# Key tiles of a graph-attention kernel: cast once and kept in DRAM, instead of cast anew in each of seven query chunks

## The chip, the cores and the metric

The kernel runs on one core of a Trainium2 chip. A core has TensorE (PE), VectorE (DVE), ScalarE (ACT), GpSimd (POOL) and SyncE (SP), each with its own in-order instruction queue; here nearly all DMAs are issued from SP's queue. Time is the device time of one execution in microseconds (us). The kernel before took 10917.11 us, the median of three runs (10916.01 to 10922.77).

## The reference

Four graph layers stand one after another over N = 3327 nodes with 128 features and a dense 0/1 adjacency matrix. The first and third multiply by the adjacency, the last adds a nearest-neighbour step. Nearly all the time is spent in the second, an attention whose logits get the adjacency added twice:

```python
h = Wq.shape[0] // d
q = (x @ Wq.T).reshape(d, n, h)
k = (x @ Wk.T).reshape(d, n, h)
v = (x @ Wv.T).reshape(d, n, h)
a = jnp.einsum('dnh,dmh->dnm', q, k) * scale
a = a + spatial_encoding + edge_encoding      # both are adj
a = jax.nn.softmax(a, axis=2)
out = jnp.einsum('dnm,dmh->dnh', a, v)
out = out.reshape(n, h * d)
return out @ Wo.T
```

With d = 128 and h = 8 there are 128 attention maps of 3327 x 3327 logits, each with a contraction over only 8 numbers: 1.4 billion exponentials.

## The kernel before, in words

**Tiling of the attention.** The queries are cut in 7 chunks of QW = 476 columns (the last has 471, worked as 472). The 128 maps are taken four at a time, which makes 32 groups. The 3327 keys are cut in T = 26 tiles of 128. One step is (chunk c, group g, tile t); the loop runs over 7 x 32 x 26 = 5824 steps with t innermost, and two steps make a pair. The order of every engine's instructions in this loop is the program's own (a manual schedule): nothing is reordered, and each queue runs ahead as far as its waits let it.

**Keys.** A product of fp32 precision is made from parts: each key row is split in a high and a low part, and four maps' parts lie on 4 x 32 partitions. In chunk 0 the class `Parting` does that on POOL for the group after next (L582, L583: `hi` and `lo`), tile by tile of t from 2 to 9, and stores the parts to DRAM (`kt` for keys, `qt` for queries). `load_keys(g)` then brings a group's keys into `k_in`, 128 partitions x 3328, with eight DMAs of 16 partitions (L606), after a memset on POOL of the last column (L601). The pool `kq` holds two such tiles. A node's place in `k_in` is node = 26 p + t, so the 128 keys of a tile t are strided, and TensorE needs the type F32R. `key_pair` (L638) therefore casts two tiles at a time from `k_in` to a small tile `k` of 128 x 2 x 128, contiguous, of which there are nine buffers; casts run seven pairs ahead of their use. This is done in all seven chunks, for the same 32 groups of keys each time. The cast is on DVE, but on POOL at t = 5, and at t = 17 where POOL has an addition to a degree sum to do (`beside`).

**A pair of steps** (`scores`). PE makes eight products of 32 x 128 by 32 x 476 (L852), four for the even tile into four `early` banks, three for the odd tile into `late` and one more `early`. DVE adds the doubled adjacency `a2` to five of them (L855, from PSUM into the tile `p8` in SBUF). For the others PE adds it in PSUM with a product by 2I (L871, one of three, two of three in chunk 0 for t below 10) or POOL multiplies by exp(a2) after the exponential (L875). ScalarE takes the exponential twice: of the three late results (L873) and of the five that DVE wrote (L876). Six steps later `weigh` multiplies with the values on PE (L883). After a group's last step DVE copies the sums `acc` to `o4` (L892, seen at t = 5 of the next group), and four DMAs store them.

**The rest of the loop.** At t = 8 the next group's queries and values are loaded (`load_rest`, L628 and L613), at t = 14 the keys of the group after the next (`load_keys`). Adjacency tiles of the next chunk are loaded at t = 6 and doubled by POOL at t = 22 (L282); each is added to a degree sum at t = 17 of the next group (L293). In group 0 of each later chunk, at t = 19, `store_sum` makes the degrees on PE (L297) after the last addition, and DVE scales them (L298). In the last group of a chunk ScalarE makes the 13 exponentials of the next chunk's odd adjacency tiles (`exp_of`).

**DMA.** SP's issues are spread in turn over eight semaphores, and each issue waits until the one eight before it has landed.

Of the kernel before, what the change touches and what calls it, by code (L numbers as in the profile page):

```python
# [8 lines left out]
F32 = mybir.dt.float32  # L9
F32R = mybir.dt.float32r  # L10
# [11 lines left out]
P = 128  # L22
N = 3327
D = 128
T = 26
NP = P * T
# [28 lines left out]
def kernel(  # L55
# [211 lines left out]
    vd = dpool.tile([GP, EA], F32, name="vd")  # L267
    ot = dpool.tile([EA, GP], F32, name="ot")
    adj16 = dpool.tile([T, P, N], BF16, name="adj16")

    q_chunks = chunks(N, QW)
    adj_pools = [ctx_at.enter_context(tc.tile_pool(name="at_adj0", bufs=T))]
# [324 lines left out]
                    self.store(side)  # L597

    def load_keys(g):
        k_in = kq.tile([P, NP], F32, name="k_in")  # L600
        nc.gpsimd.memset(k_in[:, N:], 0.0)  # L601
        for i in range(4):
            n0 = (4 * g + i) * N
            for j in range(2):
                r = 32 * i + HL * j
                nc.sync.dma_start(k_in[r : r + HL, :N], kt[:, n0 : n0 + N])  # L606
        return k_in

    def load_values(g):
        v4 = kq.tile([P, 4, T, EA], F32, name="v4")  # L610
# [119 lines left out]
    for g in range(2):  # L730
        raw = {}

        def keys(g=g, raw=raw):
            raw["k"] = kq.tile([P, NP], F32, name="k_in")
            nc.gpsimd.memset(raw["k"][:, N:], 0.0)
            load_raw(raw["k"], kf, g, N)

        def others(g=g, raw=raw):
            w = q_chunks[0][1]
            raw["q"] = side.tile([P, QW], F32, name="q_raw")  # L740
            load_raw(raw["q"], qf, g, w)
            raw["v"] = load_values(g)

        def parted(g=g, raw=raw):
            split_rows(raw["k"], raw["k"], NP, low_k)
            q4 = kq.tile([P, QW], F32R, name="q4")
            split_rows(q4, raw["q"], q_chunks[0][1], low_q)
            first.append((q4, raw["v"]))
            k_ins.append(raw["k"])

        early += [keys, others, parted]
# [77 lines left out]
    with tc.tile_pool(name="at_in", bufs=1) as a_pool, tc.tile_pool(name="at_p", bufs=4) as p_pool, tc.tile_pool(  # L829
# [16 lines left out]
        def scores(step, k, q4, a2, e_a, p8, n_g):  # L846
            c, _, t = step
            we = even(c)

            def product(i, sp, stop=True):  # L850
                r = slice(32 * i, 32 * i + 32)
                nc.tensor.matmul(sp[:, :we], k[r, t % 2, :], q4[r, :we], start=True, stop=stop)  # L852

            def add(i, sp):
                nc.vector.tensor_tensor(p8[:, PLACES[t % 2][i], :we], sp[:, :we], a2[:, :we], op=ALU.add)  # L855

            if t % 2 == 0:
                early = [ps.tile([P, 512], F32, name="early", bufs=4) for _ in range(4)]
                for i in range(4):
                    product(i, early[i])  # L860
                for i in range(4):
                    add(i, early[i])
                return
            n_i = 3 - n_g
            late = ps.tile([P, 3, 512], F32, name="late")
            early = ps.tile([P, 512], F32, name="early", bufs=4)
            for i in range(3):
                product(i, late[:, i], stop=i >= n_i)
            product(3, early)
            for i in range(n_i):  # L870
                nc.tensor.matmul(late[:, i, :we], two_i, a2[:, :we], start=False, stop=True)  # L871
            add(3, early)
            nc.scalar.activation(p8[:, 5:8, :we], late[:, :, :we], AF.Exp)  # L873
            g8 = p8[:, 8 - n_g : 8, :we]
            nc.gpsimd.tensor_tensor(g8, g8, e_a[:, :we].unsqueeze(1).to_broadcast([P, n_g, we]), op=ALU.mult)  # L875
            nc.scalar.activation(p8[:, :5, :we], p8[:, :5, :we], AF.Exp)  # L876
# [20 lines left out]
        with tc.manual_schedule(engines=engines):  # L897
# [4 lines left out]
            e_t, e_next = e_first, []  # L902
            to_store = [(0, t, a2) for t, a2 in enumerate(a_t)]
            begun, to_sum = {}, []
            for j, step in enumerate(steps):
                c, g, t = step
                n = c * n_groups + g + 1
                more = n < len(groups)
                if t == 0:
                    if j:  # L910
                        q4, v4 = coming
                        if g == 0:
                            a_t, a_next = a_next, []
                            e_t, e_next = e_next, []
                if t % 2 == 0:
                    p8 = p_pool.tile([P, 8, QW], F32, name="p8")
                parting = c == 0
                scores(step, pairs[j // 2], q4, a_t[t], e_t[t // 2], p8, 1 if parting and t < 10 else 2)
                begun[j] = (step, v4, p8)
                if j >= ahead:  # L920
                    weigh(*begun.pop(j - ahead))
                if t == 8 and more:
                    coming = first[n] if n < len(first) else load_rest(*groups[n])
                if parting:
                    if t == 0:
                        part = ahead_part
                    for due in range(t, t + 1 if t < T - 1 else max(T, 16)):
                        part.at(due)
                        if due == 15 and g + 1 < n_groups:
                            ahead_part = Parting((g + 3) % n_groups)  # L930
                            ahead_part.load(0)
                            ahead_part.load(1)

                beside = t == 17 and bool(to_sum)
                if beside:
                    while to_sum:
                        add_to_sum(*to_sum.pop(0))
                if t == 19 and g == 0 and c:
                    store_sum(c, ps.tile([P, 512], F32, name="early", bufs=4), a_pool.tile([P, QW], F32, name="o4"))
                if t % 2 and len(pairs) < len(steps) // 2:  # L940
                    key_pair(nc.gpsimd if t == ahead - 1 or beside else nc.vector, k_ins, pairs)
                if t == 14 and n + 1 < len(groups):
                    k_ins.append(load_keys(groups[n + 1][1]))
                if t == min(6, T // 2) and c + 1 < len(q_chunks):
                    for _ in range(min(len(to_store), 1 + T // n_groups)):
                        store_adj(*to_store.pop(0))
                    a_in = [load_adj(c + 1, i) for i in range(len(a_next), T * (g + 1) // n_groups)]
                if t == max(T - 4, 3) and c + 1 < len(q_chunks):
                    for a, i, w in a_in:
                        a_next.append(doubled(adj_pools[(c + 1) % 2], a[: rows_of(i), :w], i, w))  # L950
                        to_sum.append((a_next[-1], c + 1, i == 0))
                        to_store.append((c + 1, i, a_next[-1]))
                if t % 2 and g == n_groups - 1 and c + 1 < len(q_chunks):
                    e_next.append(exp_of(a_next[t], c + 1))
# [522 lines left out]
```

## Time and profile before

| what | value |
|---|---|
| median of the runs shown | 10917.11 us |
| the profiled execution's own time | 10917.88 us |
| its span in the trace | 10916.1 us, 202151 instructions |
| attention loop, first to last exponential | 432.6 to 10189 us of the span |
| PE busy | 10569.0 us (97%) |
| DVE busy | 10192.0 us (93%) |
| ACT busy | 10078.4 us (92%) |
| POOL busy | 7529.7 us (69%) |
| key loads (k_in from kt) | 1776 DMAs of 207.9 KB |
| DMA moved | 926.49 MB, 85 GB/s over the span |

A row of a group names line, engine, operation, the tiles written and read, shapes and count; behind the bar stand the busy time of the group in us, the mean of one instruction in ns, and the engine's idle time just before, with what ended it. In an extract in order of time the columns are start and duration in us, then the same names, and in brackets the idle time before with its releaser. Recorded durations of neighbours on one engine can overlap; then the distance of starts is what one costs. A matmul's busy time is not PE at its peak.

### The profile page before, as it was taken

Reading aid. Unit: us, or ns where it says so; the run is one execution under the profiler, and the core shown is the slowest. Engines: PE = TensorE matmul, PEld = TensorE weight load, DVE = VectorE, ACT = ScalarE, POOL = GpSimd, SP = SyncE. Lnnn points to the kernel's source line nnn. Section 1 sums busy time; section 2 is a strip of 40 time slices with the busy share of each in tenths; the row PEclk is TensorE's granted clock in tenths of the full one; section 3 lists DMA queues with packets and bytes.
Section 4 is the critical chain, followed back from the end, with each engine's and each line's share of the span. In section 5 each row is a group of like instructions: output and inputs, shape, how many; then the busy total and the mean of one; then the engine's idle time right before and its main releaser. Section 6 shows DMA issues by size and latency. Waiting matters only on the chain. (4 is left out here: it accounts for less than half of the span.)

```text
span 10916.1 us, 202151 instructions
## 1 busy us (share of the span) xinstructions
PE 10569.0 (97%) x76707; PEld 3105.4 (28%) x76740; DVE 10192.0 (93%) x17975; ACT 10078.4 (92%) x6276; POOL 7529.7 (69%) x4622
## 2 busy tenths in 40 slices
PE   7899999999999999999999999999999999999896
PEld 3322222222222222222222222222222222222453
DVE  5799999999999999999999999999999999999656
ACT  2799999999999999999999999999999999999432
POOL 3388887777777777777777777777777776666203
PEclk9999999999999999999999999999999999999998
DMA  8655554433433343334334333433343333333422
GB/s 299 203 126 123 122 121 110 69 63 65 71 63 63 65 72 63 63 65 71 63 65 70 64 62 65 70 65 63 64 70 64 64 60 63 56 61 60 148 101 100
DMA packets 420912, 926.49 MB, mean 85 GB/s; under 512 B 67976, under 2 KB 349567, under 8 KB 385882
## 3 DMA queue, kind: packets, MB, share of 16 engines
q1 hardware_dynamic: 416744, 906.95, 40.8%
q8 instruction: 606, 9.93, 0.4%
q0 software_dynamic: 3184, 6.51, 0.2%
q14 instruction: 378, 3.10, 0.1%
HBM read 773.47 MB, written 139.72 MB: 84 GB/s over the span
## 5 line engine op out<-in xcount | busy, mean ns | idle before, releaser
L855 DVE TENSOR_TENSOR p<-early,a 128x476 f32<-128x476 f32 (+1 forms) x14560 | 8412.0, 645 | 214.0 <-PE early L852 184.9
L875 POOL TENSOR_TENSOR p<-p,e 128x952 f32<-128x952 f32 (+2 forms) x2912 | 6325.4, 2172 | 2440.9 <-ACT p L873 2273.2
L876 ACT ACTIVATE p<-p 128x2380 f32<-128x2380 f32 (+1 forms) x2912 | 7099.5, 2438 | 0.0
L883 PE MATMUL acc<-p,v 128*9 128x476 f32 (+1 forms) x46592 | 5738.2, 564 | 28.0 <-DVE o L892 13.0
L873 ACT ACTIVATE p<-late 128x1428 f32<-128x1428 f32 (+1 forms) x2912 | 4675.3, 1606 | 33.1 <-PE late L871 30.0
L852 PE MATMUL early<-q,k 32*128 32x476 f32 (+1 forms) x14560 | 3699.5, 479 | 28.3 <-DVE p L855 5.0
L852 PEld LDWEIGHTS early<-q,k 32*128 32x128 f32 x14560 | 1567.6, 181 | 2764.0 <-DVE p L855 2708.9
L852 PE MATMUL late<-q,k 32*128 32x476 f32 (+1 forms) x8736 | 1415.9, 479 | 47.8 <-ACT p L873 47.7
L638 DVE CAST k<-k_in 128x256 fp32r<-128x256 f32 x2525 | 1335.9, 529 | 0.0
L852 PEld LDWEIGHTS late<-q,k 32*128 32x128 f32 x8736 | 547.6, 181 | 2373.2 <-ACT p L873 2156.5
L871 PE MATMUL late<-a,two_i 128*128 128x476 bf16 (+1 forms) x3072 | 1123.8, 374 | 0.0
L883 PEld LDWEIGHTS acc<-p,v 128*9 128x9 f32 x46592 | 692.5, 88 | 1351.9 <-issue 1256.4
L871 PEld LDWEIGHTS <-two_i 128*128 128x128 bf16 x3072 | 281.0, 96 | 664.8 <-issue 664.8
L638 POOL CAST k<-k_in 128x256 fp32r<-128x256 f32 x387 | 290.4, 751 | 0.0
L233 PE MATMUL agg_ps<-a,part 128*128 128x512 bf16 (+1 forms) x1067 | 226.7, 370 | 6.1 <-ACT agg L1261 3.2
L282 POOL TENSOR_SCALAR a<-a_in 128x476 bf16<-128x476 f32 (+2 forms) x156 | 225.3, 1444 | 0.5
L345 PE MATMUL agg_ps<-a,part 128*128 128x512 bf16 (+4 forms) x720 | 170.9, 395 | 51.6 <-DMA a<-in_adjT_dram 50.3
L293 POOL TENSOR_TENSOR deg_half<-deg_half,a 128x476 f32<-128x476 f32 (+1 forms) x175 | 212.4, 1213 | 2.1
L192 ACT COPY agg<-agg_ps 128x512 f32<-128x512 f32 x9 | 4.7, 594 | 196.1 <-PE agg_ps L233 196.1
L1256 PE MATMUL sp<-yT,hT 128*128 128x512 f32 (+1 forms) x364 | 171.1, 611 | 12.1 <-ACT agg L1261 6.2
L1172 POOL TENSOR_TENSOR xs_late<-xs_late,b_s 128x3328 f32<-128x3328 f32 x1 | 7.2, 7247 | 224.8 <-DVE ln_xc L162 224.8
L892 DVE COPY o<-acc 105x476 f32<-105x476 f32 (+1 forms) x224 | 144.6, 645 | 10.5 <-PE acc L883 9.1
(286 smaller groups left out, 2550.0 us busy)
## 6 DMA issues: line engine op xcount, KB each, us to landing
k_in<-kt SPq DMA_DIRECT2D x1776, 207.9 KB
v<-vd SPq DMA_DIRECT2D x896, 117.0 KB
a<-in_adjT_dram SPq DMA_DIRECT2D x39, 1663.5 KB
a<-adj SPq DMA_DIRECT2D x78, 831.8 KB
q<-qt SPq DMA_DIRECT2D x1520, 29.8 KB
a_in<-in_adjT_dram SPq DMA_DIRECT2D x125, 238.0 KB
adj<-a SPq DMA_DIRECT2D x156, 119.0 KB
vd<-v_st SPq DMA_DIRECT2D x25, 576.0 KB
```

Of the source, the lines that this page charges most:

```text
L233: nc.tensor.matmul(acc[c][:, :w], part[:, t, :], a[:, c0 : c0 + w], start=(t == 0 and i == 0), stop=(t == T - 1 and i == len(parts) - 1),)
L282: nc.gpsimd.tensor_scalar(a2[:kp, :w], a, 2.0, None, op0=ALU.mult)
L293: nc.gpsimd.tensor_tensor(deg_half[:, :w], deg_half[:, :w], a2[:, :w], op=ALU.add)
L638: engine.tensor_copy(k, slots(k_in)[:, t : t + 2, :])
L852: nc.tensor.matmul(sp[:, :we], k[r, t % 2, :], q4[r, :we], start=True, stop=stop)
L855: nc.vector.tensor_tensor(p8[:, PLACES[t % 2][i], :we], sp[:, :we], a2[:, :we], op=ALU.add)
L871: nc.tensor.matmul(late[:, i, :we], two_i, a2[:, :we], start=False, stop=True)
L873: nc.scalar.activation(p8[:, 5:8, :we], late[:, :, :we], AF.Exp)
L875: nc.gpsimd.tensor_tensor(g8, g8, e_a[:, :we].unsqueeze(1).to_broadcast([P, n_g, we]), op=ALU.mult)
L876: nc.scalar.activation(p8[:, :5, :we], p8[:, :5, :we], AF.Exp)
L883: nc.tensor.matmul(acc[32 * i : 32 * i + EA, :w], v4[:kp, i, t, :], p8[:kp, PLACES[t % 2][i], :w], start=(t == 0), stop=(t == T - 1),)
L1256: nc.tensor.matmul(sp[:, c0 : c0 + w], slots(zT)[:, t, :], z2T[:, cols], start=True, stop=False)
```

## The change

A DRAM scratch `keyd` holds, for each of the 32 groups, all 26 cast key tiles side by side (128 x 3328). In chunk 0 keys are loaded and cast as before, and each cast pair is also stored to `keyd` in one DMA of 128 rows of 1 KB, issued one pair after its cast; the seven pairs cast ahead of the loop are stored before it begins. From chunk 1 on a group's tiles come back from `keyd` in one DMA into a tile of `k_in`'s name and size, now of type F32R, issued at t = 4 of the group before; PE reads the tile t out of it directly, and `key_pair` and `load_keys` are not called. In chunk 0 the cast of t = 17 is now always on DVE.

```diff
+    keyd = dpool.tile([NH // 4, P, NP], F32, name="keyd")
 ...
-        k_in = kq.tile([P, NP], F32, name="k_in")
+        k_in = kq.tile([P, NP], F32R, name="k_in").bitcast(F32)
 ...
+    def load_tile_keys(g):
+        k = kq.tile([P, NP], F32R, name="k_in")
+        nc.sync.dma_start(k.bitcast(F32), keyd[g])
+        return k.rearrange("r (t p) -> r t p", p=P)
+
+    def store_tile_keys(n):
+        g, t = divmod(2 * n, T)
+        nc.sync.dma_start(keyd[g, :, t * P : (t + 2) * P], pairs[n].rearrange("r t p -> r (t p)").bitcast(F32))
 ...
-                nc.tensor.matmul(sp[:, :we], k[r, t % 2, :], q4[r, :we], start=True, stop=stop)
+                nc.tensor.matmul(sp[:, :we], k[r], q4[r, :we], start=True, stop=stop)
 ...
+            n_pairs = n_groups * T // 2
+            k_now, k_next = None, None
+            n_stored = len(pairs)
+            for n in range(n_stored):
+                store_tile_keys(n)
 ...
                         q4, v4 = coming
+                        k_now = k_next
 ...
-                scores(step, pairs[j // 2], q4, a_t[t], e_t[t // 2], p8, 1 if parting and t < 10 else 2)
+                k = pairs[j // 2][:, t % 2] if c == 0 else k_now[:, t]
+                scores(step, k, q4, a_t[t], e_t[t // 2], p8, 1 if parting and t < 10 else 2)
 ...
-                beside = t == 17 and bool(to_sum)
-                if beside:
+                if t == 17:
                     while to_sum:
                         add_to_sum(*to_sum.pop(0))
 ...
-                if t % 2 and len(pairs) < len(steps) // 2:
-                    key_pair(nc.gpsimd if t == ahead - 1 or beside else nc.vector, k_ins, pairs)
-                if t == 14 and n + 1 < len(groups):
+                if t % 2 and n_stored < len(pairs):
+                    store_tile_keys(n_stored)
+                    n_stored += 1
+                if t % 2 and len(pairs) < n_pairs:
+                    key_pair(nc.gpsimd if t == ahead - 1 else nc.vector, k_ins, pairs)
+                if t == 14 and n + 1 < n_groups:
                     k_ins.append(load_keys(groups[n + 1][1]))
+                if t == 4 and n_groups <= n < len(groups):
+                    k_next = load_tile_keys(groups[n][1])
```

More of the change, by code (lines that the diff above doesn't have):

```diff
@@ L733, in keys @@
         def keys(g=g, raw=raw):
-            raw["k"] = kq.tile([P, NP], F32, name="k_in")
+            raw["k"] = kq.tile([P, NP], F32R, name="k_in").bitcast(F32)
             nc.gpsimd.memset(raw["k"][:, N:], 0.0)
```

## The prediction

> **What bounds the kernel now.** I read the page first, then the sums of each engine by stretch, cut at the start of each chunk's first late exponential, then ScalarE's instructions in order of time, then DVE's and POOL's beside them. By stretch (columns: PE, weight loads, DVE, ScalarE, POOL busy us; granted clock; DMA share; GB/s), chunks 0, 1 and 6:
>
> ```profile
> 432.60:1844.30 1411.70, 1390.10 (x10531) 363.75 (x10531) 1364.77 (x2472) 1404.10 (x845) 1172.81 (x1069) 1.00 0.54 122
> 1844.30:3237.40 1393.10, 1377.63 (x10402) 372.58 (x10402) 1357.91 (x2472) 1390.52 (x846) 1034.38 (x559) 1.00 0.38 66
> 8813.70:10188.90 1375.20, 1369.30 (x10409) 371.59 (x10406) 1365.26 (x2485) 1372.60 (x833) 949.66 (x512) 1.00 0.35 56
> ```
>
> Three engines look full. Which one is, the order of time decides. The groups concerned:
>
> ```profile
> L876 ACT ACTIVATE p<-p 128x2380 f32<-128x2380 f32 (+1 forms) x2912 | 7099.5, 2438 | 0.0
> L873 ACT ACTIVATE p<-late 128x1428 f32<-128x1428 f32 (+1 forms) x2912 | 4675.3, 1606 | 33.1 <-PE late L871 30.0
> L638 DVE CAST k<-k_in 128x256 fp32r<-128x256 f32 x2525 | 1335.9, 529 | 0.0
> L638 POOL CAST k<-k_in 128x256 fp32r<-128x256 f32 x387 | 290.4, 751 | 0.0
> ```
>
> The last seven pairs of tiles have no cast, since casts run seven pairs ahead. ScalarE in chunk 6, first with casts on DVE, then without:
>
> ```profile
> 10100.03 1.95 ACT L873 ACTIVATE p<-late 128x1416 f32<-128x1416 f32 x1
> 10101.26 2.78 ACT L876 ACTIVATE p<-p 128x2360 f32<-128x2360 f32 x1
> 10103.32 1.95 ACT L873 ACTIVATE p<-late 128x1416 f32<-128x1416 f32 x1
> ...
> 10179.03 2.15 ACT L873 ACTIVATE p<-late 128x1416 f32<-128x1416 f32 x1
> 10180.26 2.98 ACT L876 ACTIVATE p<-p 128x2360 f32<-128x2360 f32 x1
> 10182.33 2.15 ACT L873 ACTIVATE p<-late 128x1416 f32<-128x1416 f32 x1
> ```
>
> Start to start a pair takes 3.29 us with the casts and 3.30 without. The starts count: recorded durations overlap. So ScalarE is the bound, at 3.319 us a pair (median spacing of L873's starts) in chunks 0 to 5 and 3.292 in the narrower chunk 6, and taking casts from DVE buys only what ScalarE loses against that floor.
>
> **What it loses.** Floor of chunks 1 to 5: 416 pairs x 3.319 = 1380.6, plus 13 more exponentials of the next chunk's tiles at 0.49 (the spacing in the last group is 3.81) = 6.4: 1387.0. Starts of the chunks give 1393.1, 1394.2, 1393.4, 1395.2, 1393.5; excess 6.1, 7.2, 6.4, 8.2, 6.5. Chunk 6: 1375.2 less 416 x 3.292 = 1369.3: 5.9. Together 40.3 us. Two parts:
>
> (a) One stall in each chunk's group 0, where PE's degree product (L297) waits for POOL's last addition and everything behind it on PE is late:
>
> ```profile
> 3267.28 1.75 ACT L873 ACTIVATE p<-late 128x1428 f32<-128x1428 f32 x1
> 3268.52 2.58 ACT L876 ACTIVATE p<-p 128x2380 f32<-128x2380 f32 x1
> 3274.19 1.36 ACT L873 ACTIVATE p<-late 128x1428 f32<-128x1428 f32 x1 [3.09 <-PE late L871]
> ```
>
> 6.91 less 3.32 = 3.59 here; over the six chunks 2.78, 3.59, 2.91, 4.75, 2.89, 3.04 = 20.0, and 0.28 each in the pairs after it, 1.6.
>
> (b) The other 18.7 us are delays of 0.1 to 0.3, mostly near t = 21. There DVE's cast meets POOL's multiplication:
>
> ```profile
> 2396.86 2.90 DVE L855 TENSOR_TENSOR p<-early,a 128x476 f32<-128x476 f32 x5
> 2399.66 1.35 DVE L638 CAST k<-k_in 128x256 fp32r<-128x256 f32 x1
> ...
> 2396.63 1.29 POOL L293 TENSOR_TENSOR deg_half<-deg_half,a 128x476 f32<-128x476 f32 x1
> 2397.86 0.68 POOL L638 CAST k<-k_in 128x256 fp32r<-128x256 f32 x1
> 2398.52 2.22 POOL L875 TENSOR_TENSOR p<-p,e 128x952 f32<-128x952 f32 x1
> ```
>
> The 964 casts of DVE with no POOL work beside them take 0.40; this one ends 0.27 after L875 does. Five additions 2.81 (start to start) and a free cast 0.33 make 3.14, 0.18 under ScalarE's 3.32; a cast of 1.35 makes 4.1.
>
> **The change part by part.** *Chunks 1 to 6, casts gone* (2525 + 387 now; 377 + 39 in the changed program). DVE falls to 2.81 a pair, slack 0.5, and part (b) should go: 18.7 at most, nothing at least; I take 17, since the late pairs are those of blocked casts. The 0.40 itself buys nothing: it lies beside ScalarE. In (a) the chain ScalarE, POOL L875, L293, PE L297 stays. Only its end shortens: in four chunks (1.44 each) DVE's cast of t = 19 sits between L298 and the additions that give PE a bank back, and PE's product waits some 0.6 for it (at 1878.81 the late products are out, the early one only at 1879.41): 4 x 0.6 = 2.4, and the 1.6 after it. Bounds 0 and 6 x 1.4 = 8.4; I take 4, from the PE row. Next late after DVE is that same stall, 16 to 20 us.
>
> *Chunks 1 to 6, the load.* Eight issues a group become one, bytes as before (1.70 MB). A 13,308-byte packet takes 1.5 us in the DMA records; 8 on each of 16 engines are 12 us. The issue waits for PE's last product on that buffer (two groups back) and stands behind the value loads, so about the group's start; PE needs it 43 us on. Behind it SP has stores and loads for the next group, up to 35 us early. Cost 0; cover 43 - 12 = 31 us. POOL loses 192 memsets of 0.1, hidden.
>
> *Chunk 0, the stores.* 416 of 131 KB (seven of them before the loop, where SP issues nothing from 427 to 442.6), each waiting on SP for a cast done a pair before. Issue: 0.35 (the row of the like adj<-a) to 0.75 (k_in<-kt), 13 a group, 4.6 to 9.8 us in SP's free stretch of about 17 (from 995 to 1012). Four stand ahead of the raw loads of the next parting: lo_k goes out at 992.8 and POOL first uses it at 1006.5, so 1.4 to 3 us later is covered. Data: 1,664 packets a group at some 0.06 (0.054 for 936 bytes) over 16 engines, 6.2 us, share 0.54 to about 0.68. A cast now waits for the store of nine pairs before, 30 us old; behind it on DVE stand the additions that ScalarE needs. The slowest backlog: the cast of t = 13 (981.1) is stored after lo_q, landing near 998, wanted at 1011. Cost 0, bounds 0 and the rival below.
>
> *Chunk 0, the cast of t = 17 moves* from POOL to DVE in 25 groups. Does it fit?
>
> ```profile
> 984.97 2.88 DVE L855 TENSOR_TENSOR p<-early,a 128x476 f32<-128x476 f32 x5
> 988.36 2.89 DVE L855 TENSOR_TENSOR p<-early,a 128x476 f32<-128x476 f32 x5 [0.52 <-PE early L852]
> ...
> 985.17 2.23 POOL L875 TENSOR_TENSOR p<-p,e 128x952 f32<-128x952 f32 x1 [1.06 <-ACT p L873]
> 988.50 2.23 POOL L875 TENSOR_TENSOR p<-p,e 128x952 f32<-128x952 f32 x1 [1.09 <-ACT p L873]
> ```
>
> DVE idles 0.52 just there, and POOL is idle too: a free cast of 0.40 hides. Bounds: -3.8 (the loss now at t = 21, 0.13 x 29, gone with POOL's shorter queue) and 25 x (1.01 - 0.52) = +12 (mean cast beside L293 and a POOL cast, 33 cases). I take 0, the row at its place. The Trainium skill, "SBUF — State Buffer", Who interferes with whom, says the port pair of the two engines is locked for a whole instruction and the other fully blocks. The casts beside L875 agree (up to 1.68). If the moved cast met L293, that rule would add up to 25 x 1.1 = 27 us and the sum would be 10924; by the idle rows it meets nothing.
>
> **Sum.** The profiled execution took 10917.9 (span 10916.1 and 1.8 around it), 0.8 over the median of 10917.1. 10917.9 - 17 - 4 + 0 = 10897.
>
> **Rivals.**
> 1. *Slower: the stores hold SP.* If SP's 13 issues and fuller engines eat the 13.7 us between lo_k's issue and its use, POOL's parting starts late; POOL has hardly a gap from 962.9 to 984, so L875 and the weighing behind it slip. Against: the six tiles (10 us) between L875 and its weighing. From 21/32 = 0.65 us a group it eats the gain; at 1.5, 10897 + 48 = 10945.
> 2. *Nothing gained:* part (b) is POOL's or PE's own and ScalarE stays as late: 10918. For it: the losses lie where POOL has extra work. Against: DVE's cast of 1.35 precedes the late pair.
> 3. *More:* all of (b), 8.4 of (a), 1.6 after it, 3.8 of chunk 0: 10917.9 - 32.5 = 10885.
>
> **How the numbers follow.** Forecast 0.63 (10890 to 10904), slower 0.12, nothing 0.13, more 0.12. 0.2% is 21.8 us, about what a measurement here can tell: faster is under 10895.3. A little under half of the forecast's share lies there: 0.30 + 0.12 = 0.42 faster; 0.33 + 0.13 = 0.46 within; 0.12 slower. The range leaves out most of the first rival and the tip of the third: 10884 to 10919.
>
> **What would show it.** Right: chunks 1 to 5 take about 1390.1 each, chunk 6 about 1372; L873's starts 3.32 apart but for one gap of 2 to 5 us a chunk; DVE there about 1190 busy instead of 1358; chunk 0 within 5 us of 1411.7, with no wait of POOL for lo tiles nor of a cast for a store. Wrong: PE waiting on the key load at a group's start, or ScalarE still late near t = 21.

## The result, and the profile after

The changed kernel took 10973.73 us (median; 10968.84 to 10977.36) beside 10919.78 (10916.01 to 10922.77) for the kernel before on the same chip: a ratio of 1.005, 95% interval 1.0035 to 1.0065, so slower by about 54 us. The forecast of 10897 has the wrong sign, and the range (10884 to 10919) doesn't hold the time. The profiled execution took 10977.36 us with a span of 10975.6; the sums below are made against that one.

By stretch (columns as before: PE, weight loads, DVE, ScalarE, POOL busy us; granted clock; DMA share; GB/s), chunks 0, 1 and 6 of the changed kernel:

```profile
433.60:1909.20 1475.60, 1430.14 (x10535) 369.14 (x10539) 1406.59 (x2490) 1407.93 (x846) 1155.47 (x1042) 0.97 0.62 153
1909.20:3300.60 1391.40, 1360.26 (x10398) 367.84 (x10390) 1220.81 (x2113) 1389.46 (x847) 988.68 (x469) 1.00 0.21 66
8872.30:10247.20 1374.90, 1354.91 (x10409) 370.29 (x10409) 1208.88 (x2109) 1372.98 (x834) 922.02 (x449) 1.00 0.17 57
```

Chunk 0 grew from 1411.7 to 1475.6, by 63.9 us; chunks 1 to 6 went from 8344.6 together to 8338.1, a gain of 6.5 where 21 was forecast. ScalarE has the same work in chunk 0 (1404 busy then, 1408 now), so it waits. Whom it waits for is in the list of waits of chunk 0 (who waited at which line for whom: us in total, times, longest). Before:

```profile
ACT p L873 <- PE late L871: 12.5, 23, 7.6
POOL hi L582 <- DMA lo_k<-kf: 4.7, 6, 1.1
```

And after (the lines of the kernel have moved by ten):

```profile
ACT p L883 <- PE late L881: 70.4, 60, 7.9
PE early L862 <- DVE p L865: 23.1, 16, 1.7
POOL hi L583 <- DMA lo_k<-kf: 29.4, 15, 2.8
```

ScalarE waits 57.9 us more for PE's last late product, PE now waits for DVE's addition, up to 1.7 us at a time, and POOL waits longer for the raw low tile `lo_k` of the next parting. These three are links of one chain.

**The first link, SP.** SP's issues in group 1 of chunk 0, in order of time, before:

```profile
503.26 5.33 SPq L606 DMA_DIRECT2D k_in<-kt  x8
509.88 0.74 SPq L575 DMA_DIRECT2D lo_k<-kf  x1
```

and after:

```profile
504.92 3.62 SPq L617 DMA_DIRECT2D keyd<-k  x2
508.64 4.84 SPq L607 DMA_DIRECT2D k_in<-kt  x8
514.66 0.74 SPq L576 DMA_DIRECT2D lo_k<-kf  x1
```

The key stores stand in SP's queue ahead of the key loads, and each issue waits until the one eight before it has landed. Counted from its group's start, the first key load went out at 26.3 us before (mean of groups 1 to 29, the first being 0) and goes out at 29.6 now; `lo_k` went out at 33.0 and now at 35.9. The DMA records show why three microseconds matter: the data of `lo_k` run on the same 16 engines behind the 12 us of the key loads. Before, its first packet started 7.4 us after its issue, at 40.4; by its semaphore it had landed at 46.1, and POOL's first `hi` was at 46.7. So the room was 0.5 us in the mean, and between 0.06 and 1.9.

**The other links, engine by engine.** Group 2 of chunk 0 before, in order of time, ScalarE, DVE and POOL:

```profile
541.17 1.37 ACT L873 ACTIVATE p<-late 128x1428 f32<-128x1428 f32 x1
544.49 1.38 ACT L873 ACTIVATE p<-late 128x1428 f32<-128x1428 f32 x1
547.83 1.36 ACT L873 ACTIVATE p<-late 128x1428 f32<-128x1428 f32 x1
...
541.98 0.75 DVE L638 CAST k<-k_in 128x256 fp32r<-128x256 f32 x1
...
540.25 2.21 POOL L875 TENSOR_TENSOR p<-p,e 128x952 f32<-128x952 f32 x1
542.62 2.23 POOL L875 TENSOR_TENSOR p<-p,e 128x952 f32<-128x952 f32 x1 [0.16 <-ACT p L873]
```

The same group after, with PE:

```profile
527.33 0.41 POOL L583 CAST hi<-lo_k 96x278 fp32r<-96x278 f32 x1 [2.73 <-DMA lo_k<-kf]
542.95 4.40 POOL L885 TENSOR_TENSOR p<-p,e 128x952 f32<-128x952 f32 x2
...
544.59 3.02 DVE L648 CAST k<-k_in 128x256 fp32r<-128x256 f32 x1
547.53 2.88 DVE L865 TENSOR_TENSOR p<-early,a 128x476 f32<-128x476 f32 x5
...
548.23 0.67 PE L862 MATMUL early<-q,k 32*128 32x476 f32 x1 [1.70 <-DVE p L865]
...
543.38 1.36 ACT L883 ACTIVATE p<-late 128x1428 f32<-128x1428 f32 x1 [0.30 <-PE late L881]
549.53 1.36 ACT L883 ACTIVATE p<-late 128x1428 f32<-128x1428 f32 x1 [2.64 <-PE late L881]
554.86 1.36 ACT L883 ACTIVATE p<-late 128x1428 f32<-128x1428 f32 x1 [1.89 <-PE late L881]
```

POOL starts its parting 2.73 us late and then works without a gap, so that its two multiplications at the end run into one stretch of 4.40 us, from 542.95 to 547.35. DVE's cast, issued into that stretch, comes out at 547.61 after 3.02 us; before, it found POOL's gap of 0.16 and took 0.75. DVE's additions follow it, PE's last early product waits 1.70 for the first of them, the product by 2I that completes `late` stands behind it on PE and is late, and ScalarE's pairs start 6.15 and 5.33 apart instead of 3.32.

The second of these, 5.33, has another cause. These two pairs and the next by stretch, columns as in the first fence:

```profile
543.38:549.53 6.15, 4.37 (x29) 1.14 (x25) 6.15 (x8) 3.50 (x3) 4.01 (x3) 0.90 0.58 188
549.53:554.86 5.33, 5.33 (x29) 0.94 (x25) 4.09 (x8) 3.44 (x3) 2.22 (x1) 0.50 0.67 224
554.86:558.19 3.33, 3.33 (x29) 0.71 (x25) 2.19 (x6) 3.33 (x2) 1.89 (x1) 0.95 1.20 186
```

In the second row PE is busy throughout with the usual 29 matmuls of a pair, but at a granted clock of 0.50: after its wait PE itself is the bound for one pair.

**The account of chunk 0.** Of groups 2 to 30, thirteen have a POOL wait of 1.5 us or more for `lo_k`. Exactly these thirteen have a cast of about 3.02 us and a PE wait of 1.69 to 1.71. They lose 5.83 us each in the mean against ScalarE's floor; the other sixteen lose 0.68, against 0.78 before. 13 x 5.83 + 16 x 0.68 - 29 x 0.78 = 64.1, the growth of chunk 0. Within a late group 2.57 us lie in the pair of the cast (6.15 above) and 2.13 in the two pairs behind it with the low clock. The late groups alternate with good ones, since a group that has lost 6 us gives the next one's loads that much more time.

### The profile page after: what moved, and what is told of

Same layout as the page of the kernel before. It is cut to its first block, busy times and chain, and to the rows that moved or that the text cites. A ratio compares the mean times of both kernels' runs of the same rounds, so it can differ in the third digit from the quotient of the medians.

```text
span 10975.6 us, 197693 instructions
## 1 busy us (share of the span) xinstructions
PE 10532.4 (96%) x76740; PEld 3090.3 (28%) x76740; DVE 9390.3 (86%) x15827; ACT 10080.1 (92%) x6276; POOL 7259.6 (66%) x4082
## 5 line engine op out<-in xcount | busy, mean ns | idle before, releaser
L886 ACT ACTIVATE p<-p 128x2380 f32<-128x2380 f32 (+1 forms) x2912 | 8284.1, 2845 | 0.0
L883 ACT ACTIVATE p<-late 128x1428 f32<-128x1428 f32 (+1 forms) x2912 | 5860.3, 2012 | 89.6 <-PE late L881 84.4
L862 PE MATMUL early<-q,k_in 32*128 32x476 f32 (+1 forms) x12480 | 2994.2, 478 | 5.4 <-DVE o L299 1.9
L862 PEld LDWEIGHTS early<-q,k_in 32*128 32x128 f32 x12480 | 1354.6, 181 | 2150.6 <-DVE p L865 2013.2
L862 PE MATMUL late<-q,k_in 32*128 32x476 f32 (+1 forms) x7488 | 1211.9, 478 | 134.1 <-ACT p L883 49.8
L862 PEld LDWEIGHTS late<-q,k_in 32*128 32x128 f32 x7488 | 469.0, 181 | 2258.4 <-ACT p L883 2241.4
L862 PE MATMUL early<-q,k 32*128 32x476 f32 x2080 | 522.8, 490 | 35.4 <-DVE p L865 28.4
L862 PEld LDWEIGHTS early<-q,k 32*128 32x128 f32 x2080 | 216.3, 185 | 435.7 <-DVE p L865 406.7
L648 DVE CAST k<-k_in 128x256 fp32r<-128x256 f32 x377 | 232.2, 616 | 0.0
L862 PE MATMUL late<-q,k 32*128 32x476 f32 x1248 | 206.1, 488 | 6.9 <-ACT p L883 6.9
L1277 PE MATMUL sp<-yT,hT 128*128 128x512 f32 (+1 forms) x364 | 171.1, 611 | 12.2 <-ACT agg L1282 6.2
```

The costliest lines, as they stand in the source:

```text
L648: engine.tensor_copy(k, slots(k_in)[:, t : t + 2, :])
L862: nc.tensor.matmul(sp[:, :we], k[r], q4[r, :we], start=True, stop=stop)
```

## The experiments

Theory A is the chain above. Its rivals were the moved cast of t = 17 (B), the stores' data as such (C), the new type or place of the key tiles (F), and, for the end of the chain, POOL's delay itself rather than the cast (D). One table for all (each ratio is to runs of the kernel before on the same chip); chunk times are the distances of the chunks' first late exponentials (chunk 6 ends one pair after its last), each in the one profiled execution; `lo_k` is its mean issue after the group's start in groups 1 to 29 of chunk 0, and a PE gap is one over 0.85 us in groups 0 to 30 of chunk 0.

| kernel | median us (range) | ratio to before (95%) | chunk 0 | chunks 1 to 6 | lo_k | PE gaps |
|---|---|---|---|---|---|---|
| before | 10919.78 | 1 | 1411.7 | 8344.6 | 33.0 | 0 |
| after | 10973.73 | 1.0050 (1.0035 to 1.0065) | 1475.6 | 8338.1 | 35.9 | 13 |
| e3_before_stores | 10975.38 (10969.07 to 10981.68) | 1.0053 (1.0036 to 1.0070) | 1465.5 | 8341.9 | 36.0 | 12 |
| e3b_before_tiny | 10945.74 (10933.06 to 10951.98) | 1.0024 (1.0015 to 1.0034) | 1439.2 | 8342.5 | 34.5 | 6 |
| e4_cast_pool | 10972.5 (10966.9 to 10989.14) | 1.0052 (1.0036 to 1.0069) | 1472.0 | 8336.0 | 36.1 | 12 |
| e1_lo_first | 10994.96 (10988.27 to 10998.62) | 1.0069 (1.0053 to 1.0086) | 1487.1 | 8340.8 | 33.3 | 20 |
| e2_stores_late | 11278.46 (11274.84 to 11291.93) | 1.0327 (1.0310 to 1.0344) | 1782.6 | 8343.2 | 33.6 | 30 |
| e8_spread | 10912.06 (10910.26 to 10918.15) | 0.9995 (0.9985 to 1.0005) | 1414.1 | 8341.3 | 34.4 | 1 |
| e5_cast_15 | 10986.17 (10978.91 to 11001.56) | 1.0058 (1.0041 to 1.0075) | 1494.2 | 8340.7 | 37.6 | 24 |
| e15_cast_11 | 10975.14 (10969.97 to 10980.52) | 1.0048 (1.0032 to 1.0063) | 1475.5 | 8340.0 | 37.8 | 4 |
| e7_weigh | 10967.3 (10965.61 to 10971.5) | 1.0046 (1.0029 to 1.0063) | 1468.1 | 8331.8 | 36.0 | 11 |
| e12_best | 10901.69 (10893.07 to 10909.78) | 0.9983 (0.9974 to 0.9992) | 1415.5 | 8321.6 | 35.7 | 1 |
| e14_before_sum | 10903.1 (10898.6 to 10912.21) | 0.9984 (0.9975 to 0.9993) | 1412.7 | 8328.1 | 33.0 | 0 |

### Only the stores, on the kernel before

e3_before_stores is the kernel before with `keyd` and the 416 stores of chunk 0 added; keys are loaded and cast as before in all chunks and `keyd` is never read.

```diff
+                if t % 2 and n_stored < min(len(pairs), n_pairs):
+                    store_tile_keys(n_stored)
+                    n_stored += 1
```

> The kernel before, with nothing of the change but the stores: chunk 0 stores each cast pair as in the change, nobody loads them, all chunks cast as before, the cast of t = 17 beside an addition stays on POOL. Theory A: the whole loss comes with the stores, chunk 0 near 1472 (1412 before) and the time near 10979. Rival B (moved cast) and rival F (the new type or place of the key tiles): the time stays near 10919.

It takes as long as the changed kernel, and chunk 0 grows by 53.8. `lo_k` goes out at 36.0; twelve groups have a cast above 2 us and lose 5.33 each. So the loss comes with the stores, and B and F fall, since neither the moved cast nor the new tiles are in this kernel. (That the product takes the type F32R is the kernel's own choice; no run tried another.) The 10 us by which chunk 0 differs from the changed kernel's are near what one chunk 0 scatters: e7 below has the changed kernel's own, and it took 1468.1 instead of 1475.6. What the change saves in chunks 1 to 6 is too small to tell the two kernels apart.

e3b_before_tiny stores 64 bytes of each row instead of 1 KB: the same issues and waits, a sixteenth of the data.

```diff
-        nc.sync.dma_start(keyd[g, :, t * P : (t + 2) * P], pairs[n].rearrange("r t p -> r (t p)").bitcast(F32))
+        nc.sync.dma_start(keyd[g, :, t * P : t * P + 16], pairs[n][:, 0, :16].bitcast(F32))
```

> As the kernel before with the stores, but each store writes only 64 bytes of each of its 128 rows, not 1 KB: the same DMAs at the same places with the same waits, a sixteenth of the bytes (keyd is not read, so the output is the reference's). Theory A in the form that SP's issue and waits push the raw loads back: lo_k is issued some 3 us late as with full stores, chunk 0 above 1450, the time above 10955. Rival C (the data): chunk 0 below 1430, the time below 10937.

The result lies between the expectations: chunk 0 grows by 27.5, half of 53.8, with `lo_k` at 34.5 and half as many PE gaps. About half of the loss comes through the issues and their order, the rest only with the data; that these act by holding the issues behind them fits the 1.5 us by which `lo_k` goes out earlier here than with full stores.

### The moved cast

e4_cast_pool gives the cast of t = 17 back to POOL where POOL has an addition to a degree sum.

```diff
-                    key_pair(nc.gpsimd if t == ahead - 1 else nc.vector, k_ins, pairs)
+                    key_pair(nc.gpsimd if t == ahead - 1 or beside else nc.vector, k_ins, pairs)
```

> The changed kernel with the cast of t = 17 back on POOL where POOL has a degree sum to add, in chunk 0. Theory A: nothing of the loss goes, since it arises at t = 11 to 15 of a group, before that cast: chunk 0 at 1475 within 10 us, the time at 10974 within 10. Rival B (the moved cast costs it): chunk 0 near 1412, the time near 10911.

Chunk 0 takes 1472.0, 3.6 less than after, and twelve groups with a cast above 2 us lose 5.79 each. Rival B falls; the forecast's zero for this part holds within the scatter of a chunk 0 (some 8 us, by e7).

### The raw loads ahead of the key loads

e1_lo_first issues `lo_k` and `lo_q` one step earlier, ahead of the key loads in SP's queue.

```diff
-                        if due == 15 and g + 1 < n_groups:
+                        if due == 14 and g + 1 < n_groups:
```

> The changed kernel with one line moved: in chunk 0 the two raw loads of the next parting (lo_k, lo_q) are issued at t = 14, ahead of the eight key loads, and not at t = 15 behind them. Theory A (the stores push these loads back on SP, behind 12 us of key data on the same engines, so POOL starts its parting 1.5 to 2.8 us late, its work runs together, and DVE's cast at t = 13 is shut out for 3.0 us): no wait of POOL for lo tiles, no cast above 1.7 us, chunk 0 falls from 1475.6 to about 1412 us, and the time to about 10911. Rival B (the moved cast of t = 17 costs it): chunk 0 stays near 1475, the time near 10974. Rival C (the stores' data slow all transfers, wherever the issue stands): chunk 0 keeps more than half of its 64 us.

The first half of the chain went as expected: POOL no longer waits for `lo_k`, which goes out at 33.3, and one group alone still has a cast above 2 us. The time did not: 21 us above the changed kernel. The list of waits of chunk 0 shows what came in its place:

```profile
DVE k L648 <- DMA keyd<-k: 57.0, 27, 5.3
POOL k L648 <- DMA keyd<-k: 58.2, 27, 5.3
```

The first key load now goes out at 37.8, not 29.6, the stores issued next to it queue behind the keys' data, and a cast may not overwrite one of the nine buffers of `k` before its store has landed. The forecast had put that wait at nothing, the store being "30 us old".

### The stores held back

e2_stores_late issues no store from t = 7 to 13 and up to two at each odd t from 15, so that nothing new stands ahead of the key loads.

```diff
-                if t % 2 and n_stored < len(pairs):
-                    store_tile_keys(n_stored)
-                    n_stored += 1
+                for _ in range(0 if t % 2 == 0 or 7 <= t <= 13 else 2 if t > 13 else 1):
+                    if n_stored < len(pairs):
+                        store_tile_keys(n_stored)
+                        n_stored += 1
```

> The changed kernel with the same stores at other places: none at t = 7 to 13, up to two at each odd t from 15 on, behind the raw loads. The data are the same, the order of key loads and raw loads as in the kernel before. Theory A (place of the stores on SP): lo_k is issued some 33 us after a group's start again, not 36; chunk 0 near 1412, the time near 10911. Rival C (the stores' data): chunk 0 stays above 1440, the time above 10940. Rival B (moved cast): near 10974.

`lo_k` goes out at 33.6 and POOL does not wait for it, but chunk 0 grows by 371 us. DVE in order of time, and then its wait in the list of chunk 0:

```profile
578.55 2.89 DVE L865 TENSOR_TENSOR p<-early,a 128x476 f32<-128x476 f32 x5 [0.16 <-PE early L862]
592.74 0.40 DVE L648 CAST k<-k_in 128x256 fp32r<-128x256 f32 x1 [11.29 <-DMA keyd<-k]
```

```profile
DVE k L648 <- DMA keyd<-k: 325.6, 30, 14.4
```

The delayed stores land behind the key loads' data, and the ring of nine buffers runs dry once a group. Both this run and e1 were misses for the same reason: each freed one load in SP's queue and counted one wait, while the stores, the key loads and the raw loads share engines.

### Room for everything

e8_spread takes what the two misses taught. The raw loads go first at t = 14, and the eight key loads go out two each at t = 14, 17, 20 and 23 instead of in one block. All stores stay.

```diff
-                        if due == 15 and g + 1 < n_groups:
+                        if due == 14 and g + 1 < n_groups:
 ...
+                if t in (14, 17, 20, 23) and n + 1 < n_groups:
+                    load_keys_of(k_ins[-1], groups[n + 1][1], (t - 14) // 3)
```

> The changed kernel with the raw loads of the next parting at t = 14, ahead of the keys, and the eight key loads of chunk 0 spread, two each at t = 14, 17, 20 and 23. In the run with the raw loads first and all eight keys behind them, POOL waited no longer for its raw tiles and no cast was above 1.0 us, but DVE's and POOL's casts waited 115 us for key stores stuck behind the keys' data (nine buffers of cast tiles, 5.3 us at most). Theory A (order on SP and behind 12 us of key data is all that costs in chunk 0): now neither wait is left, chunk 0 is 1405 to 1418 us and the time about 10911. Rival C (the stores' data or the added DMAs cost wherever they stand): chunk 0 keeps over 30 of its 64 us.

(In e1 one cast of 3.04 us was left, in group 22, which this expectation passes over.) The loss is gone. `lo_k` lands at 43.0, 3.6 us ahead of its use in the mean, and POOL waits for it twice, 0.7 us in all. Chunk 0 by stretch:

```profile
433.60:1847.70 1414.10, 1390.93 (x10535) 364.18 (x10539) 1368.31 (x2490) 1403.64 (x846) 1155.04 (x1042) 1.00 0.65 160
```

With the stores, their 55 MB and a DMA share of 0.65 (0.54 before), chunk 0 takes 2.4 us more than before. So the stores' data and issues by themselves cost no more than that; what costs is the delay that they put on the load due next. Theory A's first link is shown. The kernel as a whole is no faster than the one before.

### The end of the chain: the cast, or POOL

e5_cast_15 makes no cast at t = 13 and two at t = 15, so that DVE has none in POOL's long stretch.

```diff
-                if t % 2 and len(pairs) < n_pairs:
-                    key_pair(nc.gpsimd if t == ahead - 1 else nc.vector, k_ins, pairs)
+                for _ in range(0 if t % 2 == 0 or t == 13 else 2 if t == 15 else 1):
+                    if len(pairs) < n_pairs:
+                        key_pair(nc.gpsimd if t == ahead - 1 else nc.vector, k_ins, pairs)
```

> The changed kernel without a cast at t = 13 and with two at t = 15, in chunk 0. POOL still gets its raw tiles late. Theory A in full (the loss is DVE shut out in its cast while POOL runs two multiplications together): the 3.0 us cast is gone, at most the shorter ones of t = 9 and 11 stay, and chunk 0 falls by 30 to 60 us, the time to between 10915 and 10945. Rival D (the loss is POOL's lateness itself, through the multiplied tiles that the weighing needs): chunk 0 and the time stay where they are, 1475 and 10974.

Thirteen groups again have a POOL wait of 1.5 us or more. In the pairs 4 to 8 of the group, counted from 0, where they lost 5.31 after, they lose 0.01. But this doesn't part the cast from POOL, because these groups lose 4.49 in pairs 0 to 3 and POOL catches up meanwhile: its multiplication of pair 5 starts 1.47 us after that pair's late exponential, where it was 3.26 in the late groups of the changed kernel and 2.26 before, and in none of the thirteen do its two multiplications run together. The time was a miss, and the new wait is again that of a cast for a store:

```profile
579.64 0.40 DVE L648 CAST k<-k_in 128x256 fp32r<-128x256 f32 x1 [3.47 <-DMA keyd<-k]
```

e15_cast_11 puts the second cast at t = 11, ahead of the stretch, with two stores at t = 13.

```diff
+                for _ in range(2 if t == 13 else t % 2):
+                    if n_stored < len(pairs):
+                        store_tile_keys(n_stored)
+                        n_stored += 1
+                for _ in range(2 if t == 11 else 0 if t == 13 else t % 2):
+                    if len(pairs) < n_pairs:
+                        key_pair(nc.gpsimd if t == ahead - 1 else nc.vector, k_ins, pairs)
```

> The changed kernel with no cast at t = 13, two at t = 11 and both stored at t = 13, in chunk 0, so that no cast of t = 13 stands where POOL runs two multiplications together after a late start, and no store is held back. Theory A in full (the loss is DVE shut out in that cast): groups in which POOL waits 1.5 us or more for its raw tiles no longer lose 5.8 us, chunk 0 below 1455 and the time below 10953. Rival D (POOL's lateness itself costs, whatever DVE does): those groups go on losing 5 us or more, the time stays near 10974.

Here POOL is later than ever, in 23 of 29 groups by 1.5 us or more:

```profile
POOL hi L583 <- DMA lo_k<-kf: 72.3, 26, 5.3
```

Yet a late group loses 2.97 instead of 5.83, only five groups still have a cast above 2 us, and the PE gaps fall from 13 to 4. So the 3.02 us cast with the PE gap behind it carried about half of a late group's 5.8 us. The other 3 us remain with POOL this late, and as more groups are late the total is the same. Neither expectation holds in full. Which path the 3 us take can be read from PE's waits in chunk 0 of this kernel, here complete:

```profile
PE early L862 <- DVE p L865: 25.4, 51, 4.0
PE acc L893 <- DVE o L902: 10.9, 31, 0.4
PE late L862 <- ACT p L883: 7.7, 12, 0.8
```

The weighing (`acc`) never waits for a tile that POOL multiplies, neither here nor in the changed kernel, whose list has the same three entries. PE waits for DVE's additions 51 times instead of 16, and DVE's casts of pairs 3 and 4 last 1.07 and 1.47 us in these groups (0.64 and 0.83 before). So by the waits POOL's delay reaches ScalarE through DVE's casts here too, and the path that rival D named is not seen. What the two casts at t = 11 cost by standing together was not tried apart.

### Chunks 1 to 6: what DVE's free time buys

With the casts gone DVE is busy 1221 us a chunk instead of 1358, and the time hardly moves. Between profiled executions these chunks scatter by some us, so means say more: 8343.0 for the three kernels that cast there (before, e3, e3b) and 8340.0 for the seven that read `keyd` with nothing else changed there (after, e1, e2, e4, e5, e8, e15). The gain is about 3 us of 8343, less than the 7 us over which the seven scatter. DVE after, in a calm stretch of chunk 2, in order of time:

```profile
3839.56 2.89 DVE L865 TENSOR_TENSOR p<-early,a 128x476 f32<-128x476 f32 x5 [0.43 <-POOL p L885]
3842.88 2.90 DVE L865 TENSOR_TENSOR p<-early,a 128x476 f32<-128x476 f32 x5 [0.43 <-POOL p L885]
3846.22 2.89 DVE L865 TENSOR_TENSOR p<-early,a 128x476 f32<-128x476 f32 x5 [0.44 <-POOL p L885]
```

The starts are 3.32 to 3.34 apart. The profile names POOL, whose multiplication ends within 0.01 us of these starts in half of the cases; but in some it ends 0.2 us after DVE has started, while PE's first early product started 0.61 to 0.62 us earlier in nearly all. My reading was a ring: DVE's burst follows PE's first early product by 0.62, its five additions take 2.89, and PE's fourth early product of the next pair starts 0.05 after the fifth has freed a bank. Less the 0.24 from PE's first to its fourth early product that is 3.32 us, beside 3.326 for the median spacing of DVE's bursts and 3.319 for ScalarE's starts. But these pieces lie end to end and give the spacing whatever sets it; only breaking the ring can show it.

e7_weigh, on the changed kernel, puts the weighing of the even step ahead of the fourth early product in chunks 1 to 6, so that PE has work while it would wait.

```diff
-                for i in range(4):
+                for i in range(3):
                     product(i, early[i])
+                before_last()
+                product(3, early[3])
```

> The changed kernel with PE's order changed in chunks 1 to 6: the weighing of an even step stands before the fourth early product, not behind it. Without casts DVE's additions start 0.61 us after PE's early products each time and PE's fourth early product waits for the fifth addition (four banks), so that this ring takes 3.325 us a pair, over ScalarE's 3.319. Theory R (that ring is what keeps 14 of the 19 us of small delays): chunks 1 to 6 lose their small delays, 8338 falls to 8324 to 8330, chunk 0 stays at 1475, the time falls by 8 to 14. Rival (the small delays come from elsewhere, POOL or DMA): chunks 1 to 6 stay at 8338 within 3.

The wait is gone: the fourth early product now starts 1.1 us after the fifth addition's end, not 0.05. But DVE's bursts stay 3.326 us apart. The delays that stood alone, over 0.12 us, fall from 27 to 2, as the ring would have it, while a delay at DVE's copy of `acc` (t = 5) grows from 5.7 to 11.5 us in all; together the delays of groups 1 to 30 are 12.7 us in the changed kernel and 11.9 here. Chunks 1 to 6 fall by 6.3, less than expected, and 5.4 of that lies in group 0, where the ring was not supposed to act. So the ring is not shown to be what limits these chunks. In both kernels PE's late products start 0.05 us after ScalarE's late exponential has ended in over three quarters of the pairs, and the ends of these exponentials stand 3.326 to 3.327 apart, in the kernel before as well. What spaces them, ScalarE itself or something that feeds it, stays open.

### What the rest of the floor was worth

e14_before_sum changes one number in the kernel before: the degree product of group 0 (step (a) of the prediction) is made at t = 23 instead of 19, and no longer waits for POOL's last addition.

```diff
-                if t == 19 and g == 0 and c:
+                if t == 23 and g == 0 and c:
```

> The kernel before with the degree product at t = 23 and nothing else, to see what of the combined version's gain has nothing to do with the keys. If the stall is PE waiting for POOL's addition: chunks 1 to 6 fall from 8344 by 15 to 20 us, the time to about 10901. If it only moves: 10918.

ScalarE's waits for PE in chunks 1 to 6, less the ends, in the kernel before and then in this one:

```profile
ACT p L873 <- PE late L871: 14.9, 5, 4.3
```

```profile
ACT p L873 <- PE late L871: 3.3, 5, 0.7
```

Group 0's losses fall from 21.6 to 6.5 and the time by about 16 us, so the stall was mostly PE's wait for POOL's addition. e12_best joins this with e8 and e7:

```diff
-                if t == 19 and g == 0 and c:
+                if t == 23 and g == 0 and c:
 ...
+                if t in (14, 17, 20, 23) and n + 1 < n_groups:
+                    load_keys_of(k_ins[-1], groups[n + 1][1], (t - 14) // 3)
 ...
+                before_last()
+                product(3, early[3])
```

> The changed kernel with three things: raw loads first and key loads spread in chunk 0, the weighing before the fourth early product in chunks 1 to 6, and the degree product of group 0 at t = 23 and not at t = 19, so that PE reaches it after POOL's addition is done. From the runs so far: chunk 0 1414; chunks 1 to 6 8332 less the stalls of some 20 us that are left at t = 19, if theory A of the stall (PE waits for POOL's addition and nothing else) holds. Time near 10912 - 6 - 18 = 10888; if the stall only moves to t = 23, near 10906.

It is the fastest kernel here at 10901.69, but no faster than e14 by more than the runs scatter (0.9983, 0.9974 to 0.9992; 0.9984, 0.9975 to 0.9993). The stored keys add nothing that can be told; one moved product, without any of the change, gives the gain.

## Why the prediction was wrong, point by point

- **"Cost 0" for the stores in chunk 0: wrong, and 64 of the 80 us by which the profiled execution missed 10897.** The failed sentence is "lo_k goes out at 992.8 and POOL first uses it at 1006.5, so 1.4 to 3 us later is covered". It took the time from issue to use as cover. Of those 13.7 us 7.4 were spent in line behind the key loads' data and 5.7 from the first packet to the landing, which left 0.5 in the mean. The delay was estimated well (2.9 us in `lo_k`'s issue). The profile before has the answer: POOL already waited for `lo_k` six times, 4.7 us in all. A load that is sometimes waited for has no cover.
- **The first rival: right beginning, wrong path.** It named SP's hold on `lo_k` but priced it through POOL's multiplications and the weighing, six tiles ahead. The path went through DVE's cast, which has no such reserve, and PE's weighing never waited for POOL. It priced a late group by the delay; the runs showed 5.83 a late group, 2.2 a group in the mean, where its dearest case was 1.5.
- **A cast's wait for its store, "30 us old": right after, fragile.** It held in the changed kernel, where DVE shows no such wait in chunk 0, and failed at once in e1, e2 and e5, when stores met the key loads' data.
- **Casts gone, -17 of part (b): mis-sized.** The delays of groups 1 to 30 in chunks 1 to 6 fell from 18.1 to 12.7 us, -5.4 in this execution. The blocked casts were read rightly: pairs 10 to 12, the place near t = 21, lost 14.1 us before and 0.6 after. But the other pairs went from 4.0 to 12.1, of which 5.7 in the pair where DVE copies `acc`. The sum took all delays for delays of casts and let nothing come in their place; what sets the new ones stays open, as e7 shows.
- **Part (a), -4: wrong.** 21.6 became 20.5 in this execution, but 23.3 in the mean of the seven kernels that read `keyd` (20.5 to 25.7): nothing was gained there, and the 0.6 us that DVE's cast of t = 19 was to give back in each of four chunks don't show. The stall is PE's wait for POOL; e14 removed most of it by moving the product.
- **ScalarE as the bound, the key load hidden, the moved cast free: right.** ScalarE's pairs are still 3.319 apart where nothing disturbs them, no wait for `k_in` from `keyd` shows in chunks 1 to 6, and e4 finds no cost of the moved cast beyond the scatter of a chunk 0.
- **The account.** Forecast -21 and 0; measured -6.5 (3 by the means) and +63.9, and 2 us outside the attention loop.

## What to carry to other kernels

The cover of a load is the time from its landing to its use, read from the DMA records and from the waits, not the time from its issue; a new transfer in an in-order queue delays every load behind it, and where loads share engines, moving one earlier moves another later. A slip of a microsecond or two on an engine that is not the bound can cross a threshold: here, in the changed kernel, POOL waits of 1.06 us cost nothing and waits of 1.5 us and more cost 5.8 on ScalarE. And freeing time on an engine beside the bound buys at most what the bound loses to it; what gave a gain here was the bound's own largest wait.

## What the runs showed of the hardware

**The granted clock falls after quite short waits of PE.** Mean granted clock in the 5 us after PE took up work again, against the length of the gap before, in chunk 0 of every kernel of the table but e2 (whose gaps of 3.6 us and more are all followed by 0.50 to 0.63):

| gap of PE | gaps | granted clock in the next 5 us |
|---|---|---|
| 0.86 to 1.10 us | 7 | 1.00 in all |
| 1.20 to 1.59 us | 15 | 1.00 in eight, 0.50 to 0.69 in seven |
| 1.67 us and over | 82 | 0.50 to 0.75 in all |

e8's one gap, 1.10 us up to 976.0, by the 5 us behind it:

```profile
976.00:981.00 5.00, 5.00 (x36) 1.44 (x36) 5.00 (x9) 3.77 (x3) 4.84 (x7) 1.00 1.02 209
```

In the clock records of all these runs the clock is 1.00 or 0.50 and changes only in steps of 3.41 us. Two such steps of the changed kernel, the first with the PE wait that ended at 548.23:

```profile
544.94:548.35 3.41, 1.71 (x13) 0.43 (x12) 3.41 (x3) 1.95 (x1) 2.45 (x3) 1.00 0.50 161
548.35:551.76 3.41, 3.41 (x16) 0.61 (x17) 2.39 (x5) 2.23 (x2) 0.79 (x1) 0.50 0.54 194
```

So where a gap lies in these steps counts beside its length: of the 15 gaps of 1.20 to 1.59 us, nine lay whole in one step, and six of them were followed by the low clock; of the six that two steps shared, one was.

That is how a 1.70 us wait came to cost 4.7. The Trainium skill, "TensorE: Matmul & The Clock Gate", Part 1: The HAM clock gate, says that the array drops to half clock after an idle window of about 3.4 us. Half clock agrees with the rows of 0.50; the length does not, since here gaps of 1.23 us and up were enough, and a gap of 1.59 at another place was not. By that rule the low clock would not have come, and after would have been 13 x 2.13 = 28 us faster, an estimate.

**A waiting cast can be shut out over two instructions of POOL.** The casts of 3.02 us ended 0.26 us after POOL's second multiplication, not after the first. The Trainium skill, "SBUF — State Buffer", Who interferes with whom, says that whoever issues first has the shared port pair for the whole instruction and the other engine fully blocks; the rows agree with the blocking, and add that back-to-back instructions of POOL left no opening between them.

**The same bytes took less engine time as one load.** In the DMA records of chunks 1 to 6 the key loads from `kt`, eight transfers of 16 partitions, keep the 16 engines busy for 12.2 us a group, with packets of 13,308 bytes at a median of 1.60 us; the one load of 128 partitions from `keyd` keeps them busy for 4.7 us, with packets of 13,312 bytes at 0.50. Spread out in pairs, in chunk 0 of e8, the 16-partition packets took 1.07. The forecast had 12 us for both; how much of the difference is the crowding and how much the partitions was not tried.
